# A vision layer with a Fourier-basis key transform: keys stacked in two tiles, turns in one DRAM copy, stacked queries by two transfers

## The chip, the cores and the metric

The kernel runs on one core of one Trainium2 chip. The metric is the device time of one execution in microseconds. The core has the engines TensorE (PE, with its weight loads as PEld), VectorE (DVE), ScalarE (ACT), GpSimd (POOL) and SyncE (SP), and 16 DMA engines. All data are float32.

## The reference, cut to what matters

```python
h = einsum('bnk,ek->bne', patches(x), W) + b             # 16 images, 1024 tokens, 768 -> 256
n = layernorm(h)
q, k, v = split(n @ w_qkv)                               # 8 heads of 32
k = sum over f in 1..256 of kan_a[f]*sin(f*k) + kan_b[f]*cos(f*k)     # elementwise
h = h + softmax(q @ k.T / sqrt(32)) @ v @ w_out + b_out
n = layernorm(h)
gates = softmax(n @ gW + gb); the two largest of four, again through softmax, weigh the experts
h = h + shared_mlp(n) + sum of top-2 expert_mlp(n)
```

## The kernel before

Sixteen images of 1024 tokens go through one schedule. Of each image `keys` computes the raw keys as *turns*: the key divided by two pi, as a 32-bit integer, so that a full turn wraps by itself. It makes two rows of them for each of the 256 key features, `ui` (for the sine) and `uh` (a quarter turn on, for the cosine), and sends both to the DRAM tile `ud`. In the kernel before `ud` has the shape `[E, 2, 2, N]`: feature, sine or cosine, *copy*, token. Each row is written twice, by one transfer with a source repeated twice (line 603).

The sum over 256 frequencies is a product of slow and fast waves. A *group* is eight features; there are 32 groups in an image and 512 in all. For each group `load_waves` brings two tiles `w` of 128 partitions x 1024 from `ud` (`j` = 0, 1, four features each), by two transfers of 128 x 512 each (line 951). A row is repeated over the partitions that hold different frequencies. `load_source` brings, for eight groups at a time, the rows of `src`, which VectorE spreads into the tile `f` of the fast waves (line 991). POOL multiplies `w` and `f` with a frequency for each partition (`turn_waves`, line 1006), ACT takes the sine (`sine`, line 1016), PE mixes the slow waves by coefficients (`mix`, line 1036), VectorE multiplies with the fast ones (line 1050) and PE adds up (`add_up`, line 1069). There are eight buffers for `w`, four groups' worth.

Eight groups make the 64 features of a *pair* of heads. `finish_keys` splits their result into a rounded part and a rest and writes both to the DRAM tile `kd` (line 1088); `stack_keys` loads them into `k4`, a tile of 128 partitions x 4 x 520 that stays allocated, twice, by two transfers (line 1098). `queries` does the like with the queries: `qd` in DRAM holds the rounded part and the rest (line 640), and `stack_queries` loads them for each *attention block* (a pair and half of the queries, 128 blocks in all) into `q4`, of which there are two buffers, by four transfers of 32 partitions (line 1115). With rounded parts and rests stacked on the partitions, the scores need one matmul for each head and block of 128 keys (`score`, line 1134). ACT takes the exponential (line 1149), and PE weighs the values (`weigh`, line 1167).

The order on PE is written out by hand, as a string of letters and digits (`ORDER`): `M` is a mix, `R` an add-up, `S` a score, `W` a weighing, a digit a piece of one of four other chains of work (tokens, norms, keys, queries, projections, networks). The order on the other engines, SyncE's too, comes from a planner which runs at build time: each piece of work has a cost, a list of what it depends on, and a queue; `put(SP, "keys", 1.1, deps, ...)` is one. `transfer(3.8)` tells the planner how long a transfer keeps the DMA. These numbers are only used to lay out the order. Almost all DMAs are issued by SyncE, in that one order: when an issue must wait for a semaphore, all issues behind it wait too.

## Time and profile before

| What | Value |
|---|---|
| median of 3 runs | 3939.81 us (3923.31 to 3940.42) |
| the profiled execution's own time | 3924.07 us |
| its span | 3922.5 us |
| granted TensorE clock | 0.994 |
| PE, ACT, POOL, DVE busy | 97%, 83%, 81%, 65% |
| share of 16 DMA engines taken by SyncE's queue | 80.6%, 906.98 MB |

The page comes from one execution. Busy times are shares of the span. A group's line gives engine, operation, what it writes and reads, the count, the busy time and the mean of one in ns, and the idle time of the engine just ahead of it with what ended most of it. The rows DMA and GB/s cut the span into 40 slices. The view of waits has, for each pair, the sum in us, how often, and the longest. The view of windows gives busy times of the engines in a stretch. The trace also has a record of each DMA packet (start, duration, size, but not its engine), and of each time at which a DMA raised a semaphore.

### The profile page before, as it was taken

To read this page: it belongs to the slowest core of one execution; us is meant where nothing else is said; L and a number is where in the kernel's file an instruction comes from. 1 tells how busy PE (TensorE), PEld (TensorE's weight loads), DVE (VectorE), ACT (ScalarE), POOL (GpSimd) and SP (SyncE) were. 2 spreads that over 40 slices of the span, in tenths; PEclk is the share of its full clock that TensorE was granted. 3 is DMA by queue.
4 is the path that set the end of the run, shared out by engine and by line. 5 is a ranking of instruction groups with operands and counts; after the bars stand their busy time and mean duration, and the time that the engine had idled before them with its cause. 6 is when DMAs were issued, how large, how long until landed. Compare 5 with 4: busy or idle time off the path is not lost.

```text
span 3922.5 us, 102737 instructions
## 1 busy us (share of the span) xinstructions
PE 3810.0 (97%) x40337; PEld 1948.9 (50%) x40337; DVE 2531.7 (65%) x4075; ACT 3263.0 (83%) x3939; POOL 3193.6 (81%) x2328
## 2 busy tenths in 40 slices
PE   7899999999999999999999999999999999999998
PEld 4334454554545555455454545545455454544444
DVE  4656757667675766757667675776767767576652
ACT  2788888888888888888888888888888888888983
POOL 3998878788788878879788788878879888888860
PEclk9999999999999999999999999999999999999999
DMA  7987968888787888979889788798878889788860
GB/s 228 281 261 217 278 192 245 259 226 258 220 257 225 237 264 224 259 216 256 235 233 265 212 257 247 224 265 224 262 218 255 247 229 265 216 245 235 221 170 18
DMA packets 587615, 916.51 MB, mean 234 GB/s; under 512 B 58828, under 2 KB 177524, under 8 KB 587124
## 3 DMA queue, kind: packets, MB, share of 16 engines
q1 hardware_dynamic: 580880, 906.98, 80.6%
q8 instruction: 321, 5.26, 0.6%
q10 hardware_dynamic: 6244, 2.88, 0.3%
q14 instruction: 170, 1.39, 0.1%
HBM read 758.64 MB, written 150.99 MB: 232 GB/s over the span
## 4 chain that ended last, share of the span: by engine, by line
PE 66%; DMA 13%; ACT 8%; POOL 5%; DVE 4%; issue 3%; SPq 2%; ACTq 0%; POOLq 0%; DVEq 0%
PE av L1167 17%; PE sT L1134 10%; PE kan L1036 8%; DMA w<-ud 7%; PE red L1069 4%; PE e1p L301 3%; PE tok L301 3%; ACT w L1016 3%; POOL w L1006 3%; PE e3p L301 2%; PE tok L304 2%; DMA k<-kd 2%; PE s1p L301 2%; PE e1p L304 2%; ACT f L1016 2%
## 5 line engine op out<-in xcount | busy, mean ns | idle before, releaser
L1006 POOL TENSOR_TENSOR w<-w,lane 128x1024 int32<-128x1024 int32 x1024 | 1923.6, 1895 | 406.9 <-DMA w<-ud 275.7
L1149 ACT ACTIVATE es<-sT 128x1024 f32<-128x1024 f32 x1024 | 1014.3, 1022 | 357.3 <-PE sT L1134 312.2
L1016 ACT ACTIVATE w<-w 128x1024 f32<-128x1024 int32 x1024 | 1013.4, 1046 | 67.5 <-POOL w L1006 64.3
L1006 POOL TENSOR_TENSOR f<-f,lane 128x1024 int32<-128x1024 int32 x512 | 970.2, 1895 | 102.0 <-DVE f L991 84.8
L1134 PE MATMUL sT<-q,k 128*128 128x512 f32 x2048 | 707.6, 454 | 42.9 <-DMA k<-kd 13.4
L1050 DVE TENSOR_TENSOR f<-kan,f 128x1024 f32<-128x1024 f32 x512 | 605.2, 1214 | 203.1 <-ACT f L1016 116.3
L991 DVE STREAM_SHUFFLE f<-src 128x1024 int32<-128x1024 int32 x512 | 681.3, 1370 | 0.4
L1167 PE MATMUL av<-es,v 128*32 128x256 f32 x8192 | 638.8, 383 | 3.5 <-DVE rc L1208 2.6
L1167 PE MATMUL av<-es,ones 128*32 128x256 f32 x8192 | 630.9, 379 | 0.0
L1036 PE MATMUL kan<-w,coef 64*32 64x512 f32 x8192 | 540.1, 598 | 18.8 <-ACT w L1016 12.6
L1016 ACT ACTIVATE f<-f 128x1024 f32<-128x1024 int32 x512 | 519.0, 1046 | 4.1 <-POOL f L1006 4.1
L1134 PEld LDWEIGHTS sT<-q,k 128*128 128x128 f32 x2048 | 351.2, 190 | 340.0 <-issue 146.0
L1167 PEld LDWEIGHTS av<-es,v 128*32 128x32 f32 x8192 | 235.5, 109 | 343.2 <-issue 236.9
L1167 PEld LDWEIGHTS av<-es,ones 128*32 128x32 f32 x8192 | 267.2, 110 | 176.4 <-issue 1.4
L1191 DVE RECIPROCAL rc<-av 128x256 f32<-128x256 f32 x128 | 224.8, 1756 | 169.5 <-PE av L1167 169.5
L1036 PEld LDWEIGHTS kan<-w,coef 64*32 64x32 f32 x8192 | 129.1, 105 | 313.9 <-issue 133.4
L1069 PE MATMUL red<-f,pack 128*32 128x512 f32 x2048 | 271.0, 602 | 0.0
L301 PE MATMUL tok<-wt,x 128*128 128x256 f32 x768 | 182.1, 389 | 22.1 <-DMA w1s<-in_sW 12.5
L1016 ACT ACT_TABLE_LOAD x128 | 164.2, 1283 | 17.7 <-DMA w<-ud 15.5
L304 PE MATMUL tok<-wt,x 128*32 128x256 f32 x3072 | 178.0, 380 | 0.6 <-DVE h L548 0.6
L301 PEld LDWEIGHTS tok<-wt,x 128*128 128x128 f32 x768 | 147.4, 194 | 57.9 <-DMA w1s<-in_sW 12.4
L513 ACT ACTIVATE hn<-h,less,rstd 128x256 f32<-128x256 f32 x256 | 140.7, 591 | 39.8 <-POOL less L505 39.0
(148 smaller groups left out, 4269.5 us busy)
## 6 DMA issues: line engine op xcount, KB each, us to landing
w<-ud SPq DMA_DIRECT2D x2048, 256.0 KB
q<-qd SPq DMA_DIRECT2D x512, 128.0 KB
k<-kd SPq DMA_DIRECT2D x128, 512.0 KB
x<-in_xT SPq DMA_DIRECT2D x128, 384.0 KB
ud<-u SPq DMA_DIRECT2D x64, 512.0 KB
ud<-ui SPq DMA_DIRECT2D x64, 512.0 KB
src<-ud SPq DMA_DIRECT2D x512, 64.0 KB
qd<-qhi SPq DMA_DIRECT2D x64, 256.0 KB
```

What stands on the lines that cost most here:

```text
L301: nc.tensor.matmul(out=out, lhsT=lhsT, rhs=rhs, start=start, stop=stop)
L304: nc.tensor.matmul(out=out[ts(i, 32)], lhsT=lhsT[:, ts(i, 32)], rhs=rhs, start=start, stop=stop)
L991: nc.vector.stream_shuffle(w, sources[g // 8].rearrange("p r n -> p (r n)"), [4 * (g % 8) + i // 8 for i in range(32)],)
L1006: nc.gpsimd.tensor_tensor(w, w, f.to_broadcast([P, N]), ALU.mult)
L1016: nc.scalar.activation(x, w, AF.Sin, scale=TURN * 2.0**-32)
L1036: nc.tensor.matmul(out=ps[ds(64 * j + 32 * blk, 32), ts(r, 512)], lhsT=coef[ts(r, 64)].rearrange("p e f j -> p (e f j)"), rhs=w[ts(r, 64), ...
L1050: nc.vector.tensor_mul(w, kan.pop(g), w)
L1069: nc.tensor.matmul(out=rows_of_pair[p][ts(2 * i + r, 32), :], lhsT=pack[:, ds(PACK0 - 16 * (k % 2) - 2 * (k // 2), 32)], rhs=prod[:, ts(r, ...
L1134: nc.tensor.matmul(out=ps[:, ts(s, 512)], lhsT=k4[:, 2 * s + kc // 4, ts(kc % 4, P)], rhs=q4[:, s, :], start=True, stop=True,)
L1149: nc.scalar.activation(es, scores.pop(kc), AF.Exp, scale=SCALE)
L1167: nc.tensor.matmul(out=acc[0][ts(i, HD), ts(half, 256)], lhsT=ones32 if half else v[:, kc, p % NPAIR, ts(i % 2, HD)], rhs=es[:, ds(512 * ( ...
L1191: nc.vector.reciprocal(rc[0], acc[0][:, 256:512])
```

## The change

The DRAM tile `ud` loses its copy dimension: each row is written once, and `load_waves` reads 8 rows (four features, sine and cosine), each repeated over 16 partitions, where it read 16 rows, each repeated over 8. `load_source` reads the same rows as before from the smaller tile. The DRAM tile `qd` is laid out by block of 512 queries, with the two heads of a pair next to each other in a row; the columns of the query weights, prepared outside the kernel's device time, are permuted to match. `stack_queries` issues two transfers for a block instead of four: each brings 32 rows of 1024 elements to 64 partitions, the source standing twice in its access pattern, with the repetition as the outermost dimension. `k4` becomes two tiles, for the first and the last four blocks of 128 keys; each is loaded by its own two transfers, which depend on the last score that reads that tile, and a score waits for its own half. The planner's costs and its list of steps follow. No computing instruction is added or removed.

```diff
-    k4 = const.tile([P, 4, 520], FPR, tag="k4", name="k4")
+    k4 = [const.tile([P, 2, 520], FPR, tag=f"k4{i}", name=f"k4{i}") for i in range(2)]
...
-            st["ud"] = udp.tile([E, 2, 2, N], INT, tag="ud", name="ud")
+            st["ud"] = udp.tile([E, 2, N], INT, tag="ud", name="ud")
...
             for i, x in enumerate((uh, ui)):
-                nc.sync.dma_start(
-                    out=st["ud"][ts(rows, P), i, :, ts(blk, 512)],
-                    in_=x.unsqueeze(1).to_broadcast([P, 2, 512]),
-                )
-            done["rows", b, rows, blk] = sent(2.7, 1.2)
+                nc.sync.dma_start(out=st["ud"][ts(rows, P), i, ts(blk, 512)], in_=x)
+            done["rows", b, rows, blk] = sent(1.4, 1.0)
...
-            st["qd"] = qdp.tile([2, E, N], FP, tag="qd", name="qd")
+            st["qd"] = qdp.tile([2, 2, E, 512], FP, tag="qd", name="qd")
...
-                nc.sync.dma_start(out=st["qd"][i, ts(rows, P), ts(blk, 512)], in_=x)
+                nc.sync.dma_start(out=st["qd"][i, blk, ts(rows, P)], in_=x)
...
-            src = ud[ds(8 * (g % NG) + 4 * j, 4)].rearrange("e f i n -> (e f i) n")
+            src = ud[ds(8 * (g % NG) + 4 * j, 4)].rearrange("e f n -> (e f) n")
             for c in range(2):
-                part = src[:, ts(c, 512)].unsqueeze(1).to_broadcast([16, 8, 512])
+                part = src[:, ts(c, 512)].unsqueeze(1).to_broadcast([8, 16, 512])
                 nc.sync.dma_start(out=w[:, ts(c, 512)], in_=part)
...
-                rows = ud[ts(p % NPAIR, 64), :, 0, :].rearrange(
+                rows = ud[ts(p % NPAIR, 64)].rearrange(
                     "(g j r e) f n -> j r g e f n", j=2, r=2, e=2
                 )
...
-        deps = [("red", 4 * p + 3)] + ([("k4", p - 2)] if p > 1 else [])
+        deps = [("red", 4 * p + 3)] + ([("k4", p - 2, 1)] if p > 1 else [])
...
-    def stack_keys(p):
+    def stack_keys(p, half):
+
         def action():
-            src = rows_of_pair.pop(("k", p)).rearrange("i (d q) n -> (i d) q n", q=4)
+            src = rows_of_pair["k", p].rearrange("i (d s h) n -> h (i d) s n", s=2, h=2)[half]
             for j in range(2):
-                nc.sync.dma_start(out=k4.bitcast(FP)[ts(j, 64), :, 0:512], in_=src)
-            done["stacked", p] = transfer(3.8)
-
-        deps = [("kd", p)] + ([("score", 2 * p - 1, NT - 1)] if p > 0 else [])
-        put(SP, "keys", 1.1, deps, ("k4", p), action)
+                nc.sync.dma_start(out=k4[half].bitcast(FP)[ts(j, 64), :, 0:512], in_=src)
+            done["stacked", p, half] = transfer(1.9)
+
+        deps = [("kd", p)] + ([("score", 2 * p - 1, 4 * half + 3)] if p > 0 else [])
+        put(SP, "keys", 0.8, deps, ("k4", p, half), action)
...
             for j in range(2):
-                src = images[b]["qd"][j, ts(i, 64), ts(qb, 512)]
-                for x in range(2):
-                    nc.sync.dma_start(
-                        out=q4.bitcast(FP)[ds(64 * j + HD * x, HD), :, :],
-                        in_=src.rearrange("(s d) n -> d s n", s=2),
-                    )
+                src = images[b]["qd"][j, qb, ts(i, 64)].rearrange("(d s) n -> d (s n)", s=2)
+                nc.sync.dma_start(
+                    out=q4.bitcast(FP)[ts(j, 64)].rearrange("p s n -> p (s n)"),
+                    in_=src.unsqueeze(0).to_broadcast([2, HD, 1024]),
+                )
...
-        put(SP, "queries", 2.0, deps, ("q", att), action)
+        put(SP, "queries", 1.1, deps, ("q", att), action)
...
-                    lhsT=k4[:, 2 * s + kc // 4, ts(kc % 4, P)],
+                    lhsT=k4[kc // 4][:, s, ts(kc % 4, P)],
...
-        deps = [("stacked", att // 2), ("q4", att)]
+        deps = [("stacked", att // 2, kc // 4), ("q4", att)]
...
-        stack_keys(p)
+        for half in range(2):
+            stack_keys(p, half)
...
-    heads = np.arange(0, E, HD)[:, None]
-    arrays["wq"] = arrays["w_qkv"][:, (heads + _places()).ravel()]
+    heads = np.arange(0, E, HD).reshape(NPAIR, 1, 2)
+    arrays["wq"] = arrays["w_qkv"][:, (heads + _places()[:, None]).ravel()]
```

## The prediction

> **What bounds the kernel now.** I read the page from the top: busy shares, DMA rows, the chain; then the group with the longest wait for a DMA, SyncE's own waits and two stretches of the windows view.

> ```profile
> PE 3810.0 (97%) x40337; PEld 1948.9 (50%) x40337; DVE 2531.7 (65%) x4075; ACT 3263.0 (83%) x3939; POOL 3193.6 (81%) x2328
> DMA  7987968888787888979889788798878889788860
> q1 hardware_dynamic: 580880, 906.98, 80.6%
> HBM read 758.64 MB, written 150.99 MB: 232 GB/s over the span
> PE 66%; DMA 13%; ACT 8%; POOL 5%; DVE 4%; issue 3%; SPq 2%; ACTq 0%; POOLq 0%; DVEq 0%
> ```

> PE is busy 97%, and the chain is PE for two thirds: PE's hand-written order is the bound. The second resource is the DMA: 80.6% of all 16 engines' time on SyncE's queue. The 13% of the chain on DMA is the first crack:

> ```profile
> L1006 POOL TENSOR_TENSOR w<-w,lane 128x1024 int32<-128x1024 int32 x1024 | 1923.6, 1895 | 406.9 <-DMA w<-ud 275.7
> SPq L951 <- DMA w<-ud: 137.5, 355, 1.8
> PE sT L1134 <- DMA k<-kd: 13.4, 10, 2.4
> ```

> POOL waits 275.7 us for wave tiles; PE waits for stacked keys only 13.4. In a crowded stretch the 16 engines are full (columns: stretch, its length, busy time and count of PE, PEld, DVE, ACT, POOL, clock, DMA share, GB/s):

> ```profile
> 2550.00:2600.00 50.00, 50.00 (x460) 23.96 (x452) 39.04 (x57) 41.13 (x47) 41.49 (x25) 1.00 0.97 290
> 3260.00:3280.00 20.00, 20.00 (x172) 9.95 (x172) 15.44 (x25) 15.76 (x19) 17.88 (x12) 1.00 1.05 329
> ```

> So the reserve on the DMA is about 20% of 16 engines, and the question is what the change does to each engine's load, not to the bytes. The loads (size each):

> ```profile
> w<-ud SPq DMA_DIRECT2D x2048, 256.0 KB
> q<-qd SPq DMA_DIRECT2D x512, 128.0 KB
> k<-kd SPq DMA_DIRECT2D x128, 512.0 KB
> ud<-u SPq DMA_DIRECT2D x64, 512.0 KB
> src<-ud SPq DMA_DIRECT2D x512, 64.0 KB
> ```

> [...] between successive uses of a DMA semaphore every one of the 2048 w transfers (source 16 rows x 8 copies, destination 128) brings 16 arrivals, each of the 512 src transfers (source 8 x 4 rows, destination 32) brings 9: [...] k packets, on 64 partitions, take 153 ns in the median while alone, other uncontended 2 KB packets 84.

> **The change part by part.**

> *Turns' rows in one copy.* The two ud writes per block halve: 67 to 33.5 MB, per engine 1024 packets of 2 KB fewer at about 90 ns: 92 us of DMA time won. But the w source shrinks from 16 rows to 8, each repeated 16 times. [...] every w transfer goes to engines 0 to 7, 16 packets on each instead of 8. Nothing else covers that: engines 8 to 15 cannot help. src stays at k = 8.

> *Queries by two transfers.* 512 issues at about 419 ns become 256 on SyncE's queue, 107 us of issue less, beside other work. The source now leads with 2 copies of 32 rows of 4 KB: k = 2, engines 0 and 1, 32 rows of 4 KB on each. Before it was 32 rows outermost, k = 16. These are the engines that w fills too.

> *Keys in two tiles.* 128 loads of 512 KB become 256 of 256 KB, source 64 rows outermost, k = 16: same bytes, 128 more issues at 592 ns, 76 us of issue. Half 0 may load after score 3 of the last block, not 7: at most the 13.4 us of PE's wait are won. Each new wait stands in SyncE's one order: behind it stand the w loads, for which POOL waits. The matmuls keep shapes and number. The permuted query columns and changed planner costs only shift places in the order: I bound that by +-20 us.

> Packet prices, from the trace's packet records: 2 KB take 84 ns uncontended, 113 in the mean with only w in flight, 106 for q, 142 for k; 1 KB 48, 512 B 31. As a test, the load of a mean engine before: w 2048 x 8 x 113 = 1851; q 217; k 291; ud 184; kd 88; qd 94; src 102; out 49; x 6144 x 31 = 190; rest 80: 3146 us, 80% of the span, as the page has it.

> After, engines 0 and 1:
> - w: 2048 x 16 = 32768 packets. Bounds 84 (half the engines, less crowding) and 113 ns; I take 92: 3015 us (2753 to 3703).
> - q: 256 x 32 = 8192 packets of 4 KB. Two prices of a 2 KB packet are 168 ns; [...] I take 205: 1680 us (1311 to 2507).
> - src: 512 x 4 x 100 = 205 us (172 to 230).
> - the rest, over 16 engines, with ud halved: 92 + 88 + 291 + 94 + 49 + 190 + 80 = 884 us (830 to 1000).

> Sum 5784 us. Engines 2 to 7 have 4104, engines 8 to 15 some 880. Full stretches show a DMA share of 1.05, so packets overlap a little: 5784 / 1.05 = 5509 us. About 150 us at start and end have hardly any DMA (first w issued at 57.2 us, last at 3791.8 of 3922.5): 5659. Engine 0 also runs dry where SyncE waits: it reuses a semaphore only after the last landing on it, eight in flight, and it must see kd land before it issues k (121.1 us for kd now, over 60 times). I put 5% on that, an estimate: 5940, which I round to **5900 us**. Against it stand 3924.07 us of the profiled execution (0.4% below the median 3939.81); at this size that difference plays no part. The same sum from the low ends, without dry times, is 4950, from the high ends with 5% 7600.

> What is late next: PE, ACT and POOL keep their work (3810, 3263, 3194 us) and idle about 2000 us longer, first POOL at L1006 for w, and through it ACT and PE; eight w tiles are four groups of lookahead, which helps against jitter, not against a load above the span.

> **The rivals.**

> *Queries do not count, w does.* If the leading 2 is not what counts (the pair of dimensions carried with 32 outermost), q spreads and engines 0 to 7 carry 3015 + 205 + 884 + 217 = 4321; / 1.05, + 150, + 5% = 4480 us. [...] Against: in the same program w's pattern keeps its 16 and ud's rows their places.

> *The eight engines change from transfer to transfer* (the side that ends faster). Then w transfers in flight together cover all 16 engines and only the saving stays: 92 of 3146 us, 3% of the DMA's share of the chain (13% of 3922), 15 us, plus 13 for keys: 3895 us, 1% faster. The point that decides is whether successive k = 8 transfers share engines. For it: the trace has no engine numbers. Against: with two or more src transfers in flight and nothing else, more than 9 packets were in flight 0.4% of the time, where w reached 16 to 19; but SyncE issues src only each 652 ns, so this is weak. [...]

> *The saving is real but hidden, and the change does not do what it says to the engines*: 3920 to 3945 us.

> **How the numbers follow.** Engines 0 and 1 as bound 0.80, 5900 us; w alone on half the engines 0.09, 4480; some other slowdown from the new waits 0.03; nothing measurable 0.03; faster 0.05. Within 0.5% of 3940 is about what a measurement of this kernel can tell from no change. The range 4400 to 7000 holds most of the first case (its own bounds 4950 to 7600, of which the top needs all high ends at once) and the better half of the second. Faster 0.05, same 0.03, slower 0.92.

> **What would show it.** HBM written falls to about 117 MB and read stays at 759. DMA share of q1 falls to about half, GB/s to about 150 (873 MB in 5900 us). w transfers bring 9 arrivals each, q transfers 3. POOL's wait at L1006 for w<-ud grows from 276 us to over 1500; PE falls to about 65% busy with unchanged matmul times; SyncE waits more for landed w and q. q packets of 4 KB near 168 to 306 ns. It is wrong if w still brings 16 arrivals or the DMA share per slice stays near 0.8 with PE at 97%; if the span is near 4500 with q spread, the second case is right.

## The result, and the profile after

The changed kernel takes 5410.55 us in the median (5407.06 to 5418.6), beside 3931.56 us of the kernel before on the same chip: a ratio of 1.377, with a 95% interval of 1.3744 to 1.3796. The prediction said 5900 us and 4400 to 7000.

The page of the changed kernel, its lines for busy time, for the DMA and for the chain:

```profile
PE 4144.9 (77%) x40337; PEld 2048.5 (38%) x40337; DVE 2499.0 (46%) x4075; ACT 3290.6 (61%) x3939; POOL 3198.2 (59%) x2328
...
DMA  5544545545455454545544444454454545444441
...
q1 hardware_dynamic: 526096, 873.34, 47.7%
...
HBM read 758.64 MB, written 117.44 MB: 162 GB/s over the span
...
DMA 51%; PE 22%; ACT 7%; POOL 6%; DVE 5%; issue 4%; SPq 4%; POOLq 0%; ACTq 0%; DVEq 0%
```

Read the second and the last line together. The mean engine is busy less than half the time, where it was 80.6% before, and yet half of the chain is DMA, where it was 13%. A mean of 48% that bounds the kernel is not a spare half: some engines are full and others stand empty. The same in the view of waits, first of the computing engines and then of SyncE:

```profile
POOL w L1003 <- DMA w<-ud: 1717.7, 283, 21.8
...
PE sT L1131 <- DMA k<-kd: 426.7, 54, 20.2
```

```profile
SPq L1096 <- DMA kd<-klo: 573.8, 64, 14.3
SPq L948 <- DMA w<-ud: 352.7, 532, 2.2
SPq L967 <- DMA q<-qd: 260.9, 70, 5.9
```

POOL's wait for waves went from 275.7 to 1717.7 us. The wait for stacked keys, which the halves were to shorten, went from 13.4 to 426.7: k is not issued before kd has landed, and kd lands later. Of the 16 arrivals of a transfer of kd's rest, the last came 3.1 us after the issue in the kernel before (median of 64); in the changed kernel eight have come by 1.65 us, the next six by 3.5, and the last two come at 11.3 and 11.9. I read these as the engines that neither load fills, those that only w fills, and the two of the queries. SyncE stands at line 1096 for up to 14.3 us, with every later issue behind it: in one of the longest of these waits no issue starts between 2127.4 and 2141.6 us.

The windows view shows which engines work. The columns are those of the prediction: the stretch, its length, busy time and count of PE, PEld, DVE, ACT and POOL, the clock, the DMA share and GB/s. First a stretch of the changed kernel in which only queries are being loaded, then one with waves alone:

```profile
1230.00:1235.00 5.00, 5.00 (x80) 1.75 (x74) 4.83 (x7) 5.00 (x7) 5.00 (x4) 1.00 0.13 52
515.00:520.00 5.00, 5.00 (x56) 2.56 (x54) 3.41 (x5) 1.27 (x2) 4.71 (x5) 1.00 0.52 200
```

The shares are sixteenths in disguise: 0.13 is two engines of 16, 0.52 is eight. Two engines moved 52 GB/s, eight 200, where 16 moved 290 to 329 in the two crowded stretches of the kernel before. The packet records agree over the whole run: exactly 2 packets were in flight 16% of the time, 8 or 9 of them 47%. The arrivals at the semaphores are 9 for each of the 2048 w transfers and 3 for each of the 256 q transfers. In both the first comes 0.43 us after the issue (median); the other eight of w come from 6.2 us on, the other two of q from 13.1. With the packets in flight I read these as one for each engine: eight and two.

### The profile page after: what moved, and what is told of

Its sections match the earlier page's. It is cut to its first block, busy times and chain, and to the rows that moved or that the text cites. A ratio compares the mean times of both kernels' runs of the same rounds, so it can differ in the third digit from the quotient of the medians.

```text
span 5407.6 us, 102675 instructions
## 1 busy us (share of the span) xinstructions
PE 4144.9 (77%) x40337; PEld 2048.5 (38%) x40337; DVE 2499.0 (46%) x4075; ACT 3290.6 (61%) x3939; POOL 3198.2 (59%) x2328
## 3 DMA queue, kind: packets, MB, share of 16 engines
q1 hardware_dynamic: 526096, 873.34, 47.7%
HBM read 758.64 MB, written 117.44 MB: 162 GB/s over the span
## 4 chain that ended last, share of the span: by engine, by line
DMA 51%; PE 22%; ACT 7%; POOL 6%; DVE 5%; issue 4%; SPq 4%; POOLq 0%; ACTq 0%; DVEq 0%
DMA w<-ud 24%; DMA kd<-klo 10%; DMA k<-kd 5%; DMA q<-qd 5%; PE sT L1131 5%; PE av L1164 5%; POOL w L1003 3%; DMA ud<-ui 3%; SPq L948 2%; DMA ud<-u 2%; ACT w L1013 2%; PE red L1066 2%; PE kan L1033 2%; DMA x<-in_xT 2%; ACT es L1146 2%
## 5 line engine op out<-in xcount | busy, mean ns | idle before, releaser
L1003 POOL TENSOR_TENSOR w<-w,lane 128x1024 int32<-128x1024 int32 x1024 | 1929.3, 1894 | 1937.1 <-DMA w<-ud 1717.7
L1131 PE MATMUL sT<-q,k 128*128 128x512 f32 x2048 | 785.2, 496 | 671.0 <-DMA k<-kd 426.7
L1013 ACT ACTIVATE w<-w 128x1024 f32<-128x1024 int32 x1024 | 1028.2, 1049 | 323.0 <-POOL w L1003 300.6
L1131 PEld LDWEIGHTS sT<-q,k 128*128 128x128 f32 x2048 | 393.6, 214 | 1017.7 <-issue 601.4
L1164 PE MATMUL av<-es,v 128*32 128x256 f32 x8192 | 658.6, 395 | 50.7 <-ACT es L1146 36.3
L1033 PE MATMUL kan<-w,coef 64*32 64x512 f32 x8192 | 590.2, 619 | 86.1 <-ACT w L1013 81.8
L1164 PE MATMUL av<-es,ones 128*32 128x256 f32 x8192 | 643.5, 387 | 0.0
L1066 PE MATMUL red<-f,pack 128*32 128x512 f32 x2048 | 302.5, 663 | 0.3 <-DVE f L1047 0.3
L612 DVE CAST qhi<-q 128x512 fp32r<-128x512 f32 x64 | 44.1, 689 | 376.5 <-PE q L301 219.8
## 6 DMA issues: line engine op xcount, KB each, us to landing
w<-ud SPq DMA_DIRECT2D x2048, 256.0 KB
q<-qd SPq DMA_DIRECT2D x256, 256.0 KB
k<-kd SPq DMA_DIRECT2D x256, 256.0 KB
ud<-u SPq DMA_DIRECT2D x64, 256.0 KB
ud<-ui SPq DMA_DIRECT2D x64, 256.0 KB
qd<-qhi SPq DMA_DIRECT2D x64, 256.0 KB
```

Source lines behind the costliest of these rows:

```text
L1003: nc.gpsimd.tensor_tensor(w, w, f.to_broadcast([P, N]), ALU.mult)
L1013: nc.scalar.activation(x, w, AF.Sin, scale=TURN * 2.0**-32)
L1033: nc.tensor.matmul(out=ps[ds(64 * j + 32 * blk, 32), ts(r, 512)], lhsT=coef[ts(r, 64)].rearrange("p e f j -> p (e f j)"), rhs=w[ts(r, 64), ...
L1066: nc.tensor.matmul(out=rows_of_pair[p][ts(2 * i + r, 32), :], lhsT=pack[:, ds(PACK0 - 16 * (k % 2) - 2 * (k // 2), 32)], rhs=prod[:, ts(r, ...
L1131: nc.tensor.matmul(out=ps[:, ts(s, 512)], lhsT=k4[kc // 4][:, s, ts(kc % 4, P)], rhs=q4[:, s, :], start=True, stop=True,)
L1164: nc.tensor.matmul(out=acc[0][ts(i, HD), ts(half, 256)], lhsT=ones32 if half else v[:, kc, p % NPAIR, ts(i % 2, HD)], rhs=es[:, ds(512 * ( ...
```

## The experiments

Each is a kernel of its own; times are medians. Ratios are to the kernel before on the same chip; they are not quite the quotients of the medians. The cuts from the kernels show the lines that matter; "..." marks what is left out. The theory: each engine's load sets the time. A w source of 8 rows keeps its transfer to eight engines and the leading repeat of 2 keeps a q transfer to two, the same ones each time, and q's two are among w's eight. The main rivals: only w counts, only q counts (through the wait for kd), the layout in DRAM or the larger rows cost the time, or the halves of the keys do.

**One copy of the turns alone**, into the kernel before.

```diff
-            st["ud"] = udp.tile([E, 2, 2, N], INT, tag="ud", name="ud")
+            st["ud"] = udp.tile([E, 2, N], INT, tag="ud", name="ud")
...
-                part = src[:, ts(c, 512)].unsqueeze(1).to_broadcast([16, 8, 512])
+                part = src[:, ts(c, 512)].unsqueeze(1).to_broadcast([8, 16, 512])
...
```

> The kernel before with only the turns' rows in one copy (each w transfer reads 8 rows, each over 16 partitions). Engine-load theory: w sits on 8 engines, 32768 packets of 2 KB each at the 89 ns that the changed kernel shows: 2916 us, and q stays on 16 engines (217), src 205, the rest 884: 4222 us on engines 0 to 7. The changed kernel ran at 0.986 of such a sum (5411 of 5488), so 4160 us is the floor; PE's own order is not far below, so 4200 to 4400 us. Rival 'w alone did it': 5300 to 5450. Rival 'the queries alone did it': 3900 to 3945.

Measured: 4574.32 us, ratio 1.1657 (1.1633 to 1.168). 9 arrivals for each w transfer. Both rivals fall. The upper end of the theory's own range was 4% low; why is said below. POOL's wait for waves, 275.7 us before, is here:

```profile
POOL w L1003 <- DMA w<-ud: 763.2, 294, 10.7
```

**Both copies written, only one read.**

```diff
-            src = ud[ds(8 * (g % NG) + 4 * j, 4)].rearrange("e f i n -> (e f i) n")
+            src = ud[ds(8 * (g % NG) + 4 * j, 4), :, 0, :].rearrange("e f n -> (e f) n")
...
-                part = src[:, ts(c, 512)].unsqueeze(1).to_broadcast([16, 8, 512])
+                part = src[:, ts(c, 512)].unsqueeze(1).to_broadcast([8, 16, 512])
```

> The kernel before with both copies still written, but w reading 8 rows of the first copy, each over 16 partitions. Engine-load theory: the same load as with one copy, plus the second copy's writes, 1024 packets per engine at some 90 ns: 4314 us on engines 0 to 7, so 40 to 100 us above the one-copy kernel, 4250 to 4500. Rival 'the place or layout of ud in DRAM makes w slow, not the engines': near the kernel before, 3900 to 3960.

Measured: 4668.53 us, ratio 1.1898 (1.185 to 1.1945), again above the theory's range. The layout of `ud` is that of the kernel before, and only the read pattern differs: 8 rows by 16 partitions in place of 16 by 8. The layout isn't the cause. The step above the one-copy kernel, 94 us between the medians, is about what 1024 packets more on each engine should cost where the DMA is the bound. The 92 us of the prediction's saving are right in this place; where PE is the bound they are worth nothing, as a kernel below shows.

**The queries alone**, into the kernel before. The layout of `qd`, the order of the query columns and the planner's cost go with them, as in the change.

```diff
...
-                for x in range(2):
-                    nc.sync.dma_start(
-                        out=q4.bitcast(FP)[ds(64 * j + HD * x, HD), :, :],
-                        in_=src.rearrange("(s d) n -> d s n", s=2),
-                    )
+                nc.sync.dma_start(
+                    out=q4.bitcast(FP)[ts(j, 64)].rearrange("p s n -> p (s n)"),
+                    in_=src.unsqueeze(0).to_broadcast([2, HD, 1024]),
+                )
...
```

> The kernel before with only the queries changed: two transfers for a block, the repeat of 2 outermost. Engine-load theory: q on engines 0 and 1, 8192 packets of 4 KB at 181 ns: 1483 us, w on 16 engines 16384 packets at 95 to 113 ns: 1556 to 1851, src 205, rest 976: 4220 to 4515 us on engines 0 and 1, so 4150 to 4500 us. q transfers bring 3 arrivals, w transfers 16. Rival 'w alone did it': 3900 to 3945. Rival 'the queries alone did it, through the wait for kd behind them': 5000 to 5450.

Measured: 4830.89 us, ratio 1.231 (1.2286 to 1.2335), above the theory's range and below the third rival's. An eighth of the bytes that w moves (67 MB to 537) costs more than w does on eight engines: 904 us against 648. From the page and the waits of this kernel:

```profile
q1 hardware_dynamic: 556816, 906.95, 64.6%
```

```profile
PE sT L1133 <- DMA k<-kd: 386.2, 59, 16.3
```

The bytes are those of the kernel before (906.98 MB), the mean share is 64.6%, and the wait for keys has come without any change to the keys. If the two engines changed from transfer to transfer, this load would spread, and the kernel should hardly be slower. The packet records say so more directly. With two q transfers outstanding (issued, and not yet fully landed) and nothing else, 145 us in all, two packets were in flight for 84% of the time, and more than three for 0.1%. Two transfers on different engines would show four. They are the same two engines each time.

**The changed kernel with two copies restored.**

```diff
...
-                part = src[:, ts(c, 512)].unsqueeze(1).to_broadcast([8, 16, 512])
+                part = src[:, ts(c, 512)].unsqueeze(1).to_broadcast([16, 8, 512])
...
```

> The changed kernel with two copies restored, w again from 16 rows, each over 8 partitions. Engine-load theory: the load of the queries-only kernel, so within 1.5% of it: 4150 to 4500 us; the keys in two tiles count for nothing beside that. Rival 'w alone did it': 3900 to 3945. Rival 'the keys' halves add waits of their own': more than 2% above the queries-only kernel.

Measured: 4731.18 us, ratio 1.2055 (1.2034 to 1.2077): again above the forecast level, and 2.1% below the queries-only kernel, which was forecast to be within 1.5% of it. The halves of the keys gain where engines are short; the wait for keys, 386.2 us there, is here:

```profile
PE sT L1134 <- DMA k<-kd: 211.4, 49, 11.1
```

Two losses can now be set beside each other: one copy alone costs 648 us, the queries alone 904, the whole change 1479. That is nearly the sum, less what the halves gain. If the queries' two engines were not among the waves' eight, the whole change would cost about as much as the dearer part. So they overlap. The packet records of the changed kernel agree. With three or more w transfers outstanding and nothing else, 8 or 9 packets were in flight for 85% of the time, and more than 9 for 5%: successive w transfers share their eight engines. With queries outstanding beside them it was more than 9 for 4%, where two engines of their own would bring it to 10: the queries' two are among the eight.

**The repeat put inside the rows**, in the changed kernel: 32 rows outermost, each twice. The partitions of the stacked keys follow (rounded part and rest alternate), by a layout of `kd` with the two next to each other.

```diff
-                    in_=src.unsqueeze(0).to_broadcast([2, HD, 1024]),
+                    in_=src.unsqueeze(1).to_broadcast([HD, 2, 1024]),
...
-            kd = rows_of_pair["k", p] = kdp.tile([2, P, 512], FP, tag="kd", name="kd")
+            kd = rows_of_pair["k", p] = kdp.tile([HD, 2, 4, 512], FP, tag="kd", name="kd")
...
-                nc.sync.dma_start(out=kd[i], in_=x)
+                nc.sync.dma_start(out=kd[:, i], in_=x)
...
-            src = rows_of_pair["k", p].rearrange("i (d s h) n -> h (i d) s n", s=2, h=2)[half]
+            src = rows_of_pair["k", p].rearrange("d i (s h) n -> h (d i) s n", s=2, h=2)[half]
```

> The changed kernel with one thing turned: the repeat of a query row stands inside the rows (32 rows outermost, each twice), and the keys' rounded part and rest alternate on the partitions to match, so that a q transfer is still one of two, with the same 64 packets of 4 KB. Engine-load theory: q spreads over 16 engines, what is left is w on 8 engines, as in the one-copy kernel (4574), some 2% less for the keys in halves if that gain holds here: 4450 to 4600 us. q transfers bring 16 arrivals. Rival 'rows of 4 KB, or two transfers in place of four, cost the time': 5300 to 5420.

Measured: 4448.82 us, ratio 1.1339 (1.1314 to 1.1364). Two transfers and 64 packets of 4 KB each, as in the changed kernel, but 16 arrivals and 962 us less, at the lower edge of what was forecast. Neither the 4 KB rows nor the number of transfers is the cause: the order of two dimensions is. SyncE's wait at the same line:

```profile
SPq L1096 <- DMA kd<-klo: 311.5, 64, 8.2
```

**The keys in halves alone**, in the kernel before.

```diff
-    k4 = const.tile([P, 4, 520], FPR, tag="k4", name="k4")
+    k4 = [const.tile([P, 2, 520], FPR, tag=f"k4{i}", name=f"k4{i}") for i in range(2)]
...
```

> The kernel before with only the keys in two tiles, each loaded by its own two transfers. Engine-load theory: all transfers stay on 16 engines with the same bytes; at most the 13 us that PE waits for keys are won, and SyncE's order shifts: 3905 to 3945 us, ratio 0.995 to 1.005. Rival 'halves add waits': 3960 or more.

Measured: 3915.4 us, ratio 0.9974 (0.9964 to 0.9984): a small gain, 9 us. The score's group shows where from; before, its idle time was 42.9 us and its foremost releaser the landing of keys, 13.4 us:

```profile
L1135 PE MATMUL sT<-q,k 128*128 128x512 f32 x2048 | 709.8, 455 | 23.7 <-ACT es L1150 12.0
```

**Both mended**: the repeat inside, two copies, keys in halves.

> The same with two copies of the turns restored as well: every large transfer on 16 engines again, queries by two transfers, keys in halves. Engine-load theory: the load of the kernel before, 107 us of issue less on SyncE for the queries and some more for the keys: 3890 to 3940 us, ratio 0.99 to 1.002. Rival 'other parts of the change cost time too': 3960 or more.

Measured: 3913.62 us, ratio 0.9974 (0.9965 to 0.9983), a little faster than the kernel before and far faster than the changed one. All of the loss comes from the two read patterns. The DMA is back where it was before the change:

```profile
PE 3808.1 (97%) x40337; PEld 1948.7 (50%) x40337; DVE 2521.7 (64%) x4075; ACT 3263.7 (83%) x3939; POOL 3196.4 (82%) x2328
...
q1 hardware_dynamic: 562448, 906.97, 80.3%
```

A share of 80% runs faster than one of 48%. Beside the keys-only kernel, the queries by two transfers gain nothing that these runs can tell.

**One copy, but 16 rows read by each w transfer**, with the repeat inside. Both tiles of a group read the same 16 rows, of all eight features, so this kernel does not compute the layer; its work and bytes are the same.

```diff
...
-                part = src[:, ts(c, 512)].unsqueeze(1).to_broadcast([8, 16, 512])
+                part = src[:, ts(c, 512)].unsqueeze(1).to_broadcast([16, 8, 512])
...
```

> The kernel with the repeat inside and one copy of the turns, but each w transfer reads 16 rows of eight features, each over 8 partitions, for both tiles of a group: the keys' transform is computed of the wrong rows, the work and the bytes are the same. Engine-load theory: w on 16 engines and half the writes of turns: 3870 to 3930 us, 0 to 1% below the version with two copies. Rival 'one copy is slower to read than two, because each row is read by more partitions': 4400 to 4600.

Measured: 3915.14 us, ratio 0.998 (0.9972 to 0.9988). Writing the turns once (117.44 MB to HBM in all, in place of 150.99) gains nothing over the version with two copies. POOL waits a little less for waves, 248.9 us in place of 285.8, but PE is busy 97% in both and sets the time:

```profile
POOL w L1003 <- DMA w<-ud: 248.9, 95, 9.3
```

So the saving at which the one copy aims is worth nothing here, even where w keeps its 16 engines.

**Four rows, four engines**, in the version with both mended. Only the cosine's row of each feature is read, so this kernel does not compute the layer either.

```diff
...
-                part = src[:, ts(c, 512)].unsqueeze(1).to_broadcast([16, 8, 512])
+                part = src[:, ts(c, 512)].unsqueeze(1).to_broadcast([4, 32, 512])
...
```

> The version with both mended, but each w transfer reads only 4 rows (one copy, the cosine's row alone of each feature), each over 32 partitions: the keys' transform is computed of the wrong rows, the work and the bytes are the same. Engine-load theory: four engines per w transfer, 65536 packets of 2 KB on each of engines 0 to 3 at 88 to 100 ns: 5767 to 6554 us, src 205, q 250, the rest 976: 7200 to 7985 us of load, and at the occupancy of 0.97 to 1.01 that the other kernels show, 7100 to 8200 us; w transfers bring 5 arrivals. Rival 'what counts is whether a row is read by many partitions, in steps that level off': under 6000.

Measured: 6989.55 us, ratio 1.7809 (1.7775 to 1.7843), and 5 arrivals: the theory holds, with no levelling off. The number lies 2% below the forecast, whose packets of 88 to 100 ns were too long: they took 86. With the queries on 16 engines, the kernel takes 3914 us with w on 16 engines, 4449 on eight (there with one copy) and 6990 on four. A stretch of this kernel:

```profile
3000.00:3005.00 5.00, 2.55 (x38) 0.71 (x18) 2.36 (x2) 0.00 (x0) 2.12 (x2) 1.00 0.26 102
```

0.26 of 16 engines is four, at 102 GB/s: 25 GB/s an engine, as with two (26) and eight (25), but not with 16 in the two crowded stretches of before, where it is 18 to 21.

## Why the prediction was right

**What bounds the kernel, and that the change moves it to the DMA**: right. The likeliest case came about, with the two engines that w and q share, the prediction's 0 and 1, as the bound.

**How many engines**: right, eight for w and two for q (the prediction's k), by the arrivals. Before the result the 9 arrivals of a src transfer spoke for eight engines at 8 rows; two at a leading repeat of 2, and that transfers on few engines keep to the same ones, were the author's assumption: the trace of before shows nothing of the first and little of the second. The packets in flight, the queries-only kernel and the near-sum of the two losses show both. That they are the lowest-numbered ones, no run shows: "0 to 7" and "0 and 1" are names.

**The sum**: the mechanism was right, the sizes were high by 529 us of 5940. Two terms were priced too high. A 4 KB packet of q took 181 ns in the mean (159 in the median, 306 or more for one in twenty) where 205 was taken, an estimate between two prices of 84 and two of 153 ns: 1483 us in place of 1680. A 2 KB packet of w took 88 ns with w alone in flight, where 92 was taken: 2884 in place of 3015. With these the load of engines 0 and 1 is 2884 + 1483 + 205 + 884 = 5456 us. The rest of the miss, 201 us, lies in what was set on the sum. The division by 1.05 was right: the packet records show fewer than two packets in flight for 235 us of the span, so 5456 us of load ran in 5173, 1.055 times as fast as counted. Too high was the dry time: 150 us at the ends and 281 for SyncE's waits were put down, and the records have 121 and 114. (That engines 0 and 1 are dry in just these times is argued: what SyncE's queue puts on another engine it puts on these two as well.) So SyncE's waits empty the full engines much less than was feared. The low ends of the prediction's sum give 4975 rather than 4950, and its low end for q, 1311 us, is 160 ns a packet, less than the 168 that it names; neither slip matters here.

The experiments' forecasts for the partly loaded kernels were low because I carried the changed kernel's ratio of span to load over to them. With each kernel's own packet times, loads and spans are:

| kernel | load of its fullest engines, us | span, us |
|---|---|---|
| repeat inside | 2884 + 239 + 205 + 884 = 4212 | 4430 |
| one copy alone | 2982 + 217 + 205 + 884 = 4288 | 4557 |
| two copies restored | 1819 + 1589 + 205 + 976 = 4589 | 4714 |
| queries alone | 1851 + 1622 + 205 + 976 = 4654 | 4828 |
| the changed kernel | 5456 | 5408 |
| four rows | 5636 + 252 + 205 + 976 = 7069 | 6989 |

(The terms are w, q, src and the rest. w and q are from each trace, except that q = 217 is the prediction's; src and the rest are as in the prediction, the rest with or without the second copy. The span is that of the profiled execution.) Where the load is a few hundred us above the 3900 that PE's order needs, 125 to 269 us come on top; far above it, nothing does. For the two kernels with only the queries on two engines, the packet records show what this is: 362 us (two copies restored) and 407 us (queries alone) with fewer than two packets in flight, beside 235 in the changed kernel. The fullest engines run dry more often there. The likely reason, argued and not tested, is that near to balance the two bounds take turns, stretch by stretch.

**The parts costed at little**: 13.4 us at most for the keys, measured 9 us alone, in the kernel before; but 100 us in the kernel short of engines, which the prediction did not foresee. The 92 us of DMA time from single writes gave nothing on the path.

**What would show it**: HBM written 117.44 MB (117 foretold), read unchanged, share of the queue 47.7% (about half), POOL's wait 1717.7 us (over 1500). Wrong was PE at 65% with unchanged matmul times: PE is busy 77%. The 3810 us of before would be 70% of the span, shorter than predicted; the rest comes from matmuls that got longer.

**The rivals**: w alone at 4480 us falls by the 3 arrivals of q; as a kernel of its own (the repeat inside) it came out at 4449. The rival that ended faster, with engines that change, falls by the one-copy kernel, 648 us slower than the kernel before. Even with w on all 16 engines its 15 us for the saved writes did not appear.

## What to carry to other kernels

Before repeating or reshaping a transfer, look at the outermost dimension of its source: here 8 rows repeated 16 times left half of the DMA engines empty (9 arrivals in place of 16, 648 us), and a repeat of 2 on the outside nearly all of them (3 arrivals, 904 us). A copy more in DRAM or another partition order can be the cheaper way: with both, the kernel took 3914 us. Judge a DMA by its fullest engine: a falling mean share (80.6 to 47.7%) with growing waits for landings (275.7 to 1717.7 us for waves) was here the mark of transfers on few engines, and the count of arrivals at a semaphore told how many: 3, 5 and 9 for two, four and eight. A saving of bytes was worth its packets here only where the DMA was the bound (94 us), and nothing where PE was (3915 us beside 3914).

## What was not expected of the hardware

Matmuls got slower where PE had to wait. The mean of a score's matmul is 454 ns before, 496 in the changed kernel and in the one with four rows, and the granted clock over the span is 0.994, 0.885 and 0.805 of full speed. The two lines of the group, of the changed kernel and of the mended one:

```profile
L1131 PE MATMUL sT<-q,k 128*128 128x512 f32 x2048 | 785.2, 496 | 671.0 <-DMA k<-kd 426.7
```

```profile
L1134 PE MATMUL sT<-q,k 128*128 128x512 f32 x2048 | 706.9, 454 | 22.9 <-ACT es L1149 12.8
```

Also, an engine moved w's packets faster when fewer engines ran them: a w packet took 113 ns with w alone on 16 engines, 88 on eight, 86 on four. With half the engines, less than half the rate was lost: 200 GB/s in the stretch above, where 16 engines moved 290 to 329 in the crowded stretches. That is no ceiling of 16 engines: two stretches of 5 us of the kernel before, with turns being written beside w, have 380 and 385.
